# Scores of the first attention layer: eight 32x64 tiles of TensorE in place of four 32x128 tiles

## The chip, the cores and the metric

The kernel runs on one core of a Trainium2 chip. The metric is the device time of one execution in microseconds, and the median of several runs is compared. All data is float32.

## What is computed

The input is a batch of 8 images with 32x32 positions and 512 channels. Two residual attention layers follow each other. The first has 16 heads of 32 channels, the second 4 heads of 128 channels with relative position logits. The change concerns the first layer alone:

```python
# layer 0, N = 1024 tokens, 16 heads of 32 channels
x = x + _L0_conv_ref(_gn(x), w_qkv, w_proj, b_proj)

qkv = xt @ w_qkv
q, k, v = ...                                  # each (B, 16, N, 32)
attn = jnp.einsum('bhid,bhjd->bhij', q * 32 ** -0.5, k)   # the scores
attn = jax.nn.softmax(attn, axis=-1)
out = jnp.einsum('bhij,bhjd->bhid', attn, v)
out = out.transpose(...).reshape(B, N, C) @ w_proj + b_proj
```

## The kernel before

Activations are held transposed, with channels on the 128 partitions and the 1024 tokens along the free dimension. The 512 channels are four chunks of 128, and one chunk holds four heads of the first layer, each on 32 partitions of its own.

The attention of the first layer (`attention_0`) walks through `steps`: four chunks `m`, two halves `h` of 512 queries, and eight blocks `j` of 128 keys. That is 64 steps for an image and 512 steps in all. One step has two parts.

- `front` computes the scores of four heads (`HB` = 4) for 128 keys by 512 queries. Head `r` takes its channels from partitions 32r to 32r+31, so its matmul (line 522) uses 32 rows and all 128 columns of TensorE, and it writes its own PSUM bank `ps[:, r, :]`. The four heads occupy the four row groups of the array. Then one ScalarE exponential (line 530) reads all four banks and writes `e`. The `ps` tile of four banks exists once (`bufs=1`), so the scores of the next step wait for the exponential of this one.
- `back` belongs to the step before. It multiplies `e` by the values (line 541): four matmuls with 128 rows and 32 columns, one for each head, which together fill the 128 partitions of one accumulator `acc`. VectorE adds `e` into a running sum (lines 550 and 552). At the end of a row of eight blocks, `finish` forms the sums over the keys with four matmuls of 128 rows by 32 columns (line 562), and `normalise` divides.

The rest of TensorE's work is put between these steps by `side_by_side`: projections of this image, of the next one and of the last one, through `by_columns` (line 305). It cuts every projection into four matmuls of 128 rows by 32 columns, one for each column group of the array:

```python
for g in range(P // 32):
    columns = slice(32 * g, 32 * g + 32)
    ins = nc.tensor.matmul(
        out[columns, :], weights[:, columns], moving, ...
```

The position logits of the second layer (lines 598 and 605) are of the same shape of tile. The attention of the second layer (lines 637, 638 and 649) uses the whole array of 128 by 128 and stands in stretches of its own.

TensorE's order of instructions is thus: scores of a step (line 522), values of the step before (line 541), one or two projections (line 305), and again scores. In the profile a float32 matmul stands as two MATMUL records, each with a weight load (LDWEIGHTS, engine PEld) of its own: the four score matmuls of a step are eight records.

Of the kernel before, what the change touches and what calls it, by code (L numbers as in the profile page):

```python
# [17 lines left out]
P = 128  # L18
# [9 lines left out]
def quick_path(  # L28
# [23 lines left out]
    nc = tc.nc  # L52
# [5 lines left out]
    NB = 512  # L58
    NH = N // NB
    D0 = 32  # L60
    H1, D1 = 4, 128
    HB = P // D0
# [39 lines left out]
    for u in range(4):  # L102
        rows = slice(32 * u, 32 * u + 32)
# [378 lines left out]
    def normalise(dst, acc_sums, name):  # L482

        su = mem.tile([P, NB], F32, tag="rec", name=f"su_{name}", bufs=2)
        nc.scalar.copy(su, acc_sums)  # L488
        turned = mem.tile([P, NB], F32, tag="rec", name=f"tu_{name}", bufs=2)
        nc.vector.transpose(turned, su)  # L490
        few = turned.rearrange("p (t c) -> p t c", c=32)[:, :, 0]
        rec = mem.tile([P, NB // 32], F32, tag="few", name=f"rc_{name}", bufs=2)
        nc.vector.reciprocal(rec, few)
        at = check_at[0]
        check_at[0] += 1
        nc.vector.tensor_tensor_reduce(
            out=few,
            in0=few,
            in1=rec,
            op0=ALU.add,  # L500
            op1=ALU.max,
            scale=1.0,
            scalar=0.0,
            accum_out=checks[:, at : at + 1],
        )
        nc.vector.transpose(  # L506
            su.rearrange("p (t c) -> p t c", c=32),
            rec.unsqueeze(2).to_broadcast([P, NB // 32, 32]),
        )
        nc.gpsimd.tensor_tensor(dst, dst, su, op=ALU.mult)  # L510

    def attention_0(q, k, v, b):

        steps = [(m, h, j) for m in (0, 2, 1, 3) for h in range(NH) for j in range(NT)]
        state = {}

        def front(m, h, j):
            name = f"0_{b}_{m}_{h}_{j}"
            ps = psum.tile([P, HB, NB], F32, tag="ps", name=f"ps_{name}", bufs=1)
            for r in range(HB):  # L520
                rows = slice(r * D0, (r + 1) * D0)
                nc.tensor.matmul(  # L522
                    ps[:, r, :],
                    k[m][rows, j * P : (j + 1) * P],
                    q[m][rows, h * NB : (h + 1) * NB],
                    start=True,
                    stop=True,
                )
            e = mem.tile([P, HB, NB], F32, tag="e0", name=f"e_{name}", bufs=2)
            nc.scalar.activation(e, ps, AF.Exp, scale=D0 ** -0.5)  # L530
            return e

        def back(m, h, j, e):
            name = f"0_{b}_{m}_{h}_{j}"
            if j == 0:
                state["acc"] = psum.tile([P, NB], F32, tag="acc", name=f"acc_{name}", bufs=1)
                state["first"] = e
            acc = state["acc"]
            for r in range(HB):
                c0 = (m * HB + r) * D0  # L540
                nc.tensor.matmul(  # L541
                    acc[r * D0 : (r + 1) * D0, :],
                    v[:, j, c0 : c0 + D0],
                    e[:, r, :],
                    start=(j == 0),
                    stop=(j == NT - 1),
                )
            if j == 1:
                state["esum"] = mem.tile([P, HB, NB], F32, tag="es0", name=f"es_{name}", bufs=1)
                nc.vector.tensor_add(state["esum"], state["first"], e)  # L550
            elif j > 1:
                nc.vector.tensor_add(state["esum"], state["esum"], e)  # L552
            if j < NT - 1:
                return
            nc.scalar.copy(q[m][:, h * NB : (h + 1) * NB], acc)
            state["ended"] = (m, h, state["esum"])

        def finish(m, h, esum):
            name = f"0_{b}_{m}_{h}"
            su = psum.tile([P, NB], F32, tag="acc", name=f"sums_{name}", bufs=1)  # L560
            for r in range(HB):
                nc.tensor.matmul(  # L562
                    su[r * D0 : (r + 1) * D0, :],
                    ones[:, :D0],
                    esum[:, r, :],
                    start=True,
                    stop=True,
                )
            normalise(q[m][:, h * NB : (h + 1) * NB], su, name)

        pending = None
        for at in steps:
            if "ended" in state:
                finish(*state.pop("ended"))
            e = front(*at)
            if pending is not None:
                back(*pending)
            pending = (*at, e)
            yield 2
        back(*pending)  # L580
        yield 1
        finish(*state.pop("ended"))
# [832 lines left out]
```

## Time and profile before

| What | Value |
|---|---|
| Median of 5 runs | 3923.36 us (3921.57 to 3928.71) |
| Profiled execution, time | 3921.98 us |
| Profiled execution, span | 3920.1 us |
| Mean granted TensorE clock | 0.996 |
| Busy: TensorE matmul / weight load | 3810.7 us / 1415.5 us |
| Busy: VectorE / ScalarE / GpSimd | 2523.0 / 1721.9 / 615.6 us |
| Line 522, scores | 4096 matmul records, 590.7 us busy |
| Line 541, values | 4096 matmul records, 548.6 us busy |
| Line 530, exponential | 512 instructions, 961.9 us busy |

The page's first part gives the time in which each engine was busy, and its share of the span. PE is the matmul and PEld the weight load, which has an engine row of its own because it can run beside a matmul. Part 5 groups instructions by line and shape. A shape such as `32*128` means 32 rows by 128 columns of the array. The number after the bar is the busy time of the whole group as a union of its records, then the mean duration of one record in ns. Records that run at the same time each count with their full duration in the mean, so the mean times the count is more than the busy time. The timeline merges neighbouring records of a kind: it gives the start, the length from the first start to the last end, and the count.

### The profile page before, as it was taken

What the parts mean: (1) busy time and instruction counts of PE and PEld (TensorE: products, weight loads), DVE (VectorE), ACT (ScalarE), POOL (GpSimd) and SP (SyncE); (2) the same over time, 40 slices, a digit from 0 to 9 for tenths busy, and PEclk for the clock granted to TensorE, in tenths of its full rate; (3) what the DMA queues carried; (4) which work ended last, traced back from release to release, by engine and by line L of the source; (5) the groups of instructions that cost most, each with busy time, mean ns of one, the idle gap of its engine ahead of it and who ended that gap; (6) DMA issues with size and microseconds to landing.
All of it is one profiled execution on the core that took longest, in us unless ns stands there. A gap on an engine that the chain in (4) does not pass through costs nothing.

```text
span 3920.1 us, 71583 instructions
## 1 busy us (share of the span) xinstructions
PE 3810.7 (97%) x30338; PEld 1415.5 (36%) x30338; DVE 2523.0 (64%) x2915; ACT 1721.9 (44%) x1761; POOL 615.6 (16%) x396
## 2 busy tenths in 40 slices
PE   6999899999999999999999999999999999999998
PEld 3222244232443324432343323433234332344353
DVE  5777775577745867458664686656865568654544
ACT  1555553444434454344544445344453445643232
POOL 1341001121111210112101121111200112011101
PEclk9999999999999999999999999999999999999999
DMA  6231120133201422023120241103311123110401
GB/s 167 72 110 41 47 60 6 39 115 70 60 2 53 116 59 55 10 89 84 46 54 16 92 94 38 44 24 97 88 44 32 31 91 69 31 63 21 120 17 23
DMA packets 498694, 234.18 MB, mean 60 GB/s; under 512 B 286368, under 2 KB 478144, under 8 KB 497344
## 3 DMA queue, kind: packets, MB, share of 16 engines
q1 hardware_dynamic: 495232, 214.79, 20.5%
q0 software_dynamic: 2608, 13.70, 0.9%
q8 instruction: 241, 3.95, 0.4%
q10 hardware_dynamic: 528, 1.05, 0.1%
q14 instruction: 85, 0.70, 0.1%
HBM read 170.72 MB, written 58.72 MB: 59 GB/s over the span
## 4 chain that ended last, share of the span: by engine, by line
PE 85%; DVE 8%; ACT 3%; issue 2%; POOL 1%; DMA 1%; SPq 1%; DVEq 0%; POOLq 0%; ACTq 0%
PE ps L522 12%; PE ps L637 11%; PE acc L649 11%; PE acc L541 10%; PE y_k L305 4%; PE y_q L305 4%; PE y_v L305 4%; PE ps L638 3%; PE x_v L305 3%; PE z_k L305 3%; PE x_k L305 3%; PE x_q L305 3%; PE z_v L305 3%; PE z_q L305 3%; ACT e L530 2%; DVE es L552 2%
## 5 line engine op out<-in xcount | busy, mean ns | idle before, releaser
L530 ACT ACTIVATE e<-ps 128x2048 f32<-128x2048 f32 x512 | 961.9, 1879 | 842.2 <-PE ps L522 643.1
L552 DVE TENSOR_TENSOR es<-es,e 128x2048 f32<-128x2048 f32 x384 | 888.3, 2313 | 402.8 <-ACT e L530 400.5
L522 PE MATMUL ps<-q,k 32*128 32x512 f32 x4096 | 590.7, 642 | 33.4 <-ACT e L530 33.2
L640 ACT ACTIVATE e<-ps 128x512 f32<-128x512 f32 x512 | 305.7, 597 | 586.4 <-PE ps L638 549.9
L541 PE MATMUL acc<-e,v 128*32 128x512 f32 x4096 | 548.6, 607 | 0.4 <-ACT su L488 0.4
L637 PE MATMUL ps<-q,k 128*128 128x512 f32 x1024 | 523.8, 593 | 0.3 <-DVE posT L623 0.3
L649 PE MATMUL acc<-e,v 128*128 128x512 f32 x1024 | 522.0, 593 | 0.0
L660 DVE TENSOR_TENSOR es<-es,e 128x512 f32<-128x512 f32 x384 | 291.6, 759 | 265.0 <-ACT e L640 263.7
L510 POOL TENSOR_TENSOR q<-q,su 128x512 f32<-128x512 f32 x128 | 214.3, 1674 | 1567.9 <-DVE su L506 1567.1
L638 PE MATMUL ps<-posT,sel 128*128 128x512 f32 x512 | 406.9, 795 | 0.0
L522 PEld LDWEIGHTS ps<-q,k 32*128 32x128 f32 x4096 | 161.7, 183 | 428.9 <-ACT e L530 213.3
L637 PEld LDWEIGHTS ps<-q,k 128*128 128x128 f32 x1024 | 194.0, 190 | 245.7 <-issue 240.2
L649 PEld LDWEIGHTS acc<-e,v 128*128 128x128 f32 x1024 | 193.6, 190 | 146.2 <-issue 104.8
L541 PEld LDWEIGHTS acc<-e,v 128*32 128x32 f32 x4096 | 81.9, 108 | 385.7 <-issue 341.2
L550 DVE TENSOR_TENSOR es<-e,e 128x2048 f32<-128x2048 f32 x64 | 175.1, 2735 | 38.9 <-ACT e L530 38.9
L490 DVE STREAM_TRANSPOSE tu<-su 128x512 f32<-128x512 f32 x128 | 90.6, 708 | 135.9 <-ACT su L488 135.7
L638 PEld LDWEIGHTS ps<-posT,sel 128*128 128x128 f32 x512 | 97.5, 190 | 122.2 <-issue 122.2
L488 ACT COPY su<-sums 128x512 f32<-128x512 f32 x128 | 74.9, 585 | 149.5 <-PE sums L562 81.5
L658 DVE TENSOR_TENSOR es<-e,e 128x512 f32<-128x512 f32 x64 | 44.2, 690 | 145.7 <-ACT e L640 145.7
L623 DVE TENSOR_TENSOR posT<-pp,posT 32x512 fp32r<-32x512 f32 x128 | 111.8, 873 | 32.0 <-ACT posT L618 30.7
L618 ACT CAST posT<-pp 32x512 fp32r<-32x512 f32 x128 | 105.9, 827 | 45.1 <-PE pp L605 43.9
L414 POOL TENSOR_TENSOR k<-b_k,p_k 128x512 f32<-128x512 f32 x32 | 50.6, 1583 | 477.3 <-ACT p_k L379 477.3
(188 smaller groups left out, 4507.7 us busy)
## 6 DMA issues: line engine op xcount, KB each, us to landing
w_qkv<-ws_qkv SPq DMA_DIRECT2D x168, 128.0 KB, 2.5
xs<-in_x SPq DMA_DIRECT2D x256, 64.0 KB, 2.5
d<-x0T SPq DMA_DIRECT2D x32, 512.0 KB, 3.4
x1T<-d SPq DMA_DIRECT2D x32, 512.0 KB, 5.1
d<-x1T SPq DMA_DIRECT2D x32, 512.0 KB, 3.4
x2T<-d SPq DMA_DIRECT2D x32, 512.0 KB, 5.6
out<-ot SPq DMA_DIRECT2D x256, 64.0 KB, 2.0
w_qkv<-in_L_conv_w_qkv SPq DMA_DIRECT2D x126, 128.0 KB, 2.2
```

The costliest lines, as they stand in the source:

```text
L305: ins = nc.tensor.matmul(out[columns, :], weights[:, columns], moving, start=start, stop=stop, skip_group_check=open_sum,)
L510: nc.gpsimd.tensor_tensor(dst, dst, su, op=ALU.mult)
L522: nc.tensor.matmul(ps[:, r, :], k[m][rows, j * P : (j + 1) * P], q[m][rows, h * NB : (h + 1) * NB], start=True, stop=True,)
L530: nc.scalar.activation(e, ps, AF.Exp, scale=D0 ** -0.5)
L541: nc.tensor.matmul(acc[r * D0 : (r + 1) * D0, :], v[:, j, c0 : c0 + D0], e[:, r, :], start=(j == 0), stop=(j == NT - 1),)
L550: nc.vector.tensor_add(state["esum"], state["first"], e)
L552: nc.vector.tensor_add(state["esum"], state["esum"], e)
L637: nc.tensor.matmul(ps, k[h][:, keys], q[:, h, queries], start=True, stop=False)
L638: nc.tensor.matmul(ps, sel[:, keys], posT[:, h, queries], start=False, stop=True)
L640: nc.scalar.activation(e, ps, AF.Exp, scale=1.0 / math.sqrt(D1))
L649: nc.tensor.matmul(acc, v[:, j, h * D1 : (h + 1) * D1], e, start=(j == 0), stop=(j == NT - 1),)
L660: nc.vector.tensor_add(state["esum"], state["esum"], e)
```

## The change

Each head's 128 keys are taken in two halves of 64. The score matmul of a head becomes two, each with 32 rows and 64 columns of the array, which write partitions 0 to 63 and 64 to 127 of the same PSUM bank. The first halves of all four heads are issued first, then the second halves. Operands, results and the exponential after them are the same.

```diff
@@ -517,15 +517,18 @@
         def front(m, h, j):
             name = f"0_{b}_{m}_{h}_{j}"
             ps = psum.tile([P, HB, NB], F32, tag="ps", name=f"ps_{name}", bufs=1)
-            for r in range(HB):
-                rows = slice(r * D0, (r + 1) * D0)
-                nc.tensor.matmul(
-                    ps[:, r, :],
-                    k[m][rows, j * P : (j + 1) * P],
-                    q[m][rows, h * NB : (h + 1) * NB],
-                    start=True,
-                    stop=True,
-                )
+            for i in range(2):
+
+                some = slice(64 * i, 64 * i + 64)
+                for r in range(HB):
+                    rows = slice(r * D0, (r + 1) * D0)
+                    nc.tensor.matmul(
+                        ps[some, r, :],
+                        k[m][rows, j * P + 64 * i : j * P + 64 * i + 64],
+                        q[m][rows, h * NB : (h + 1) * NB],
+                        start=True,
+                        stop=True,
+                    )
             e = mem.tile([P, HB, NB], F32, tag="e0", name=f"e_{name}", bufs=2)
             nc.scalar.activation(e, ps, AF.Exp, scale=D0 ** -0.5)
             return e
```

## The prediction

> **What bounds the kernel now.** I read the page's first part, then the chain that ended last, then the groups of instructions, then the timeline of one ordinary step.
>
> ```profile
> PE 3810.7 (97%) x30338; PEld 1415.5 (36%) x30338; DVE 2523.0 (64%) x2915; ACT 1721.9 (44%) x1761; POOL 615.6 (16%) x396
> ...
> PE 85%; DVE 8%; ACT 3%; issue 2%; POOL 1%; DMA 1%; SPq 1%; DVEq 0%; POOLq 0%; ACTq 0%
> ```
>
> TensorE is busy in 97% of the span and carries 85% of the chain that ended last. Nothing else comes near: VectorE has 64%. So what a step of scores costs on TensorE passes into the time nearly whole. But "busy" is not "streaming at full rate", and the groups show where it is not:
>
> ```profile
> L522 PE MATMUL ps<-q,k 32*128 32x512 f32 x4096 | 590.7, 642 | 33.4 <-ACT e L530 33.2
> ...
> L541 PE MATMUL acc<-e,v 128*32 128x512 f32 x4096 | 548.6, 607 | 0.4 <-ACT su L488 0.4
> ...
> L522 PEld LDWEIGHTS ps<-q,k 32*128 32x128 f32 x4096 | 161.7, 183 | 428.9 <-ACT e L530 213.3
> ...
> L541 PEld LDWEIGHTS acc<-e,v 128*32 128x32 f32 x4096 | 81.9, 108 | 385.7 <-issue 341.2
> ```
>
> Scores (L522) and values (L541) have the same count of matmul records of the same 512 columns, yet a score record is 35 ns longer in the mean. The two weight-load rows give the reason: a load of 128 columns takes 183 ns, one of 32 columns 108 ns. TensorE idled only 33 us before the scores for the exponential (L530), in 28 places; in the other steps `ps` is free in time.
>
> The timeline of TensorE, start and length in us, shows an ordinary step:
>
> ```profile
> 1307.35 0.61 PE L305 MATMUL z_wp<-q,w_p 128*32 128x512 f32 x4
> 1307.89 1.14 PE L522 MATMUL ps<-q,k 32*128 32x512 f32 x8
> 1308.96 1.07 PE L541 MATMUL acc<-e,v 128*32 128x512 f32 x8
> 1309.85 1.90 PE L305 MATMUL x_wp<-q,w_p 128*32 128x512 f32 x16
> ```
>
> and its weight loads:
>
> ```profile
> 1307.89 0.31 PEld L522 LDWEIGHTS ps<-q,k 32*128 32x128 f32 x8 [0.84 <-issue]
> 1308.96 0.16 PEld L541 LDWEIGHTS acc<-e,v 128*32 128x32 f32 x8 [0.76 <-issue]
> 1309.42 0.13 PEld L305 LDWEIGHTS x_wp<-q,w_p 128*32 128x32 f32 x4 [0.30 <-issue]
> 1309.85 0.13 PEld L305 LDWEIGHTS x_wp<-q,w_p 128*32 128x32 f32 x4 [0.30 <-issue]
> ```
>
> From the start of the scores to the start of the values are 1.07 us; from there to the projection, with as many records, only 0.89. The projection's loads return every 0.43 us, four at a time: that is one round, four column groups streaming 512 columns together. A step's scores and values are two such rounds each, 0.86 us. What lies above it is set-up.
>
> The single records of this step take the 1.07 us apart. The four first-pass matmuls last 692 ns, the four second-pass ones 588. The difference, 104 ns, is the first load of 128 columns, which nothing covers: the tile shape changes here from 128x32 to 32x128, and nothing of the new shape starts until the old one has drained. The second passes start 534 ns after the first ones: 427 of streaming and 107 of load. Neighbouring tiles start 7 ns apart, so the fourth is 20 ns behind the first. From the end of the last stream to the first load of the values pass another 88 ns, the drain. Sum: 107 + 427 + 427 + 20 + 88 = 1069, against 1071 read in nearly all 512 steps. For the values the same calculation gives 27 ns of open load (matmul records of 617 and 592), and no drain at the end because the projection has the same tile shape.
>
> **The change part by part.** It touches one line. The order of the instructions of the changed kernel has eight matmuls of 64x512 where four of 128x512 stood, in 512 steps. On TensorE, ScalarE and GpSimd all else keeps its order; on VectorE one statistics instruction changes places with a neighbour; on SyncE's queue a few loads of `xs`, issued four in a row, move past one other transfer each. There are no new waits or transfers, and ScalarE reads the same four banks behind the last matmul. So the sum has three terms, each times 512.
>
> 1. Streaming. Eight tiles of 32x64 fill the array as four of 32x128 did. If all eight stream together, a step is still two rounds of 427 ns: nothing gained or lost. The trace has four row tiles together (L522) and four column tiles together (L541, L305), but no shape cut both ways. Bounds: 0 if rows and columns are independent; two more rounds and a load, about 0.85 to 0.9 us a step, if the two halves of a head follow each other. I take 0. The Trainium skill ("TensorE: Matmul & The Clock Gate", Part 3) has a rule that speaks against it: a weight load overlaps running matmuls only where its row group differs. Each second-half tile has the row group of a first half, so by that rule its load would wait for that matmul, and the step would lose some 0.88 us, 450 us in all. The trace contradicts the rule: L541's four tiles share all 128 rows and differ in columns alone, and their eight loads are done within 0.16 us while the first matmuls have been running since 1308.96. The same part gives a 4x4 packing as 10.6 times faster than single tiles, which speaks for tiles cut both ways; no run here shows it.
>
> 2. The open load. It falls from 128 to 64 columns. By the rows: (183 - 108) / 96 = 0.78 ns a column, so 50 ns less; by the open part, 107 for 128 columns and 27 for 32 is 0.83 a column, so 53 less. Bounds: 0 (the two halves of a row group load one after the other) and -54. I take -53, for L541 shows four column tiles loading side by side: -53 x 512 = -27.1 us. The second-pass loads lie under the first streams and cost nothing before or after; their cover is 427 ns for some 130 ns.
>
> 3. The stagger. Eight tiles begin 7 ns apart, so the last is 47 ns behind the first, not 20, and the drain waits for it: +27 x 512 = +13.8 us. Bounds: 0 (the drain hides it) and twice the step between tiles, 13 ns, +73 a step. The row for it: four projection loads of about 110 ns span 0.13 us, so three steps make 0.02. The skill states a floor ("TensorE: Matmul & The Clock Gate", Part 1): starts of matmuls are never closer than about 25 ns. With it eight starts would take 175 ns, four 75, and the sum of terms 2 and 3 would be +47 a step, +24 us: slower. The records of L522 start 7 ns apart, so I take 7.
>
> The supply of instructions is not a limit by the trace: the scores become 32 records in about 1.04 us, and a projection with 256 columns (x_v, y_v in L305) takes 64 records in 1.73 us without a gap, 27 ns each.
>
> Sum: 0 - 27.1 + 13.8 = -13.3 us. In the 28 steps that wait for the exponential the loop is scores, exponential, scores, and shorter scores shorten it just as much, so nothing is taken off. The profiled execution took 3921.98 (span 3920.1): 3921.98 - 13.3 = 3908.7. The median of the runs stands 1.4 above it, so about 3910 is expected. About 0.2%, 8 us, is what a measurement of this kernel can tell from no change.
>
> **The rivals.**
>
> A, the forecast (0.65): all eight tiles together. Between 3895 (term 2 whole, stagger hidden) and 3920. For it: the free mixing of column tiles in L541 and L305. Against: no mixed tile is in the trace.
>
> B, the halves follow each other (0.18): the two tiles of a row group share one stream of `q`, or one load path, so the second half starts when the first has passed. Place: between i = 0 and i = 1 of line 522. Price: two rounds and a load of 64 columns, 854 + 53, less the 53 saved at the start, so 854 x 512 = +437 us: 4361. Scores would then bind TensorE by two more rounds a step, while ScalarE's exponential, 1.88 us a step, stays hidden. It decides from the point where the last tile starts more than 74 ns behind the first (53 saved and the 20 there are now). For it: a row group has so far never been used by two tiles at once; against: in L541 all row groups are, by four.
>
> C, no gain (0.17): the loads of the two halves share the row group's path, or tiles start up to 13 ns apart. Terms 2 and 3 cancel or turn to +20 ns a step: 3918 to 3934. For it: the stagger takes back half the gain as it is.
>
> That the change doesn't do what it says is excluded by the order of the instructions. VectorE as the new bound is excluded as well: a gain of 0.3% leaves it at 64%.
>
> **How the numbers follow.** The likeliest is A: 3910. The range 3893 to 3934 holds A and C, 0.82 of the chance, and leaves B out. Faster by over 0.2%: most of A and none of B, 0.60. Within: the edge of A and half of C, 0.13. Slower: the rest of C and B, 0.27.
>
> **What would show it.** Right: weight loads of L522 near 133 ns, 8192 of them; first-pass matmuls about 53 ns longer than second-pass ones, not 104; scores to values in 1.04 us, not 1.07; the eight first passes starting within 50 ns. Wrong: two groups of starts 0.4 us or more apart, scores to values near 1.9 us (B); or loads still near 183 ns or starts 13 ns apart (C).

## Result and profile after

The changed kernel takes 3915.95 us (median of 28 runs, 3910.45 to 3919.30), the kernel before 3922.91 us (48 runs, 3918.68 to 3928.71). The ratio is 0.9982 with a 95% interval of 0.9977 to 0.9987: about 7 us faster, with an interval from 5 to 9. The forecast was 13 us faster by 3910, in a range of 3893 to 3934. The direction is right and the size is half.

The page of the changed kernel, engines and the groups of the scores (now L525), of the values (L544) and of their weight loads:

```profile
span 3917.2 us, 79775 instructions
...
PE 3803.6 (97%) x34434; PEld 1370.8 (35%) x34434; DVE 2524.4 (64%) x2915; ACT 1722.1 (44%) x1761; POOL 616.5 (16%) x396
...
L525 PE MATMUL ps<-q,k 32*64 32x512 f32 x8192 | 578.0, 616 | 35.3 <-ACT e L533 35.2
...
L544 PE MATMUL acc<-e,v 128*32 128x512 f32 x4096 | 548.1, 607 | 0.4 <-ACT su L488 0.4
...
L525 PEld LDWEIGHTS ps<-q,k 32*64 32x64 f32 x8192 | 120.5, 130 | 432.1 <-ACT e L533 215.4
```

Twice as many score records as before take 578 us of TensorE in place of 591. A load of 64 columns takes 130 ns, which lies between the 183 of 128 columns and the 108 of 32. TensorE is still the bound.

The timeline of the same step as in the prediction, matmuls and then weight loads:

```profile
1308.25 0.61 PE L305 MATMUL z_wp<-q,w_p 128*32 128x512 f32 x4
1308.79 1.11 PE L525 MATMUL ps<-q,k 32*64 32x512 f32 x16
1309.84 1.06 PE L544 MATMUL acc<-e,v 128*32 128x512 f32 x8
1310.72 1.90 PE L305 MATMUL x_wp<-q,w_p 128*32 128x512 f32 x16
```

```profile
1308.79 0.23 PEld L525 LDWEIGHTS ps<-q,k 32*64 32x64 f32 x16 [0.84 <-issue]
1309.84 0.16 PEld L544 LDWEIGHTS acc<-e,v 128*32 128x32 f32 x8 [0.81 <-issue]
```

Scores to values are 1.05 us here, 1.07 before. All sixteen score loads are done within 0.23 us, so both halves of every head have their weights long before the first streams end. The single records give the sum exactly. In the middle of the run the eight first-pass matmuls start 2 to 49 ns after the first load, the eight second passes 480 ns behind the first ones (534 before), and the values 564 ns after that (537 before). Together this is 1044 ns against 1071, in practically every step that no wait or other work interrupts. Over 512 steps, 26.7 ns are 13.7 us.

So the scores gained what was forecast, and about half of it does not arrive in the time. Note also where the step stands: at 1308.79 in this profile, 0.9 us later than in the profile of before. By then 196 shorter steps had passed, which alone would have put it 5.2 us earlier. The experiments ask two things: whether the three terms of the step are what they were taken for, and where the rest went.

### The profile page after: what moved, and what is told of

Its sections match the earlier page's. It is cut to its first block, busy times and chain, and to the rows that moved or that the text cites. A ratio compares the mean times of both kernels' runs of the same rounds, so it can differ in the third digit from the quotient of the medians.

```text
span 3917.2 us, 79775 instructions
## 1 busy us (share of the span) xinstructions
PE 3803.6 (97%) x34434; PEld 1370.8 (35%) x34434; DVE 2524.4 (64%) x2915; ACT 1722.1 (44%) x1761; POOL 616.5 (16%) x396
## 3 DMA queue, kind: packets, MB, share of 16 engines
q10 hardware_dynamic: 528, 1.05, 0.1%
## 4 chain that ended last, share of the span: by engine, by line
PE 84%; DVE 9%; ACT 3%; issue 2%; POOL 1%; DMA 1%; SPq 0%; another core or an unknown queue 0%; DVEq 0%; ACTq 0%; POOLq 0%
PE ps L640 11%; PE acc L652 11%; PE ps L525 11%; PE acc L544 10%; PE y_k L305 4%; PE y_q L305 4%; PE y_v L305 4%; PE ps L641 3%; PE x_v L305 3%; PE z_k L305 3%; PE x_k L305 3%; PE x_q L305 3%; PE z_v L305 3%; PE z_q L305 2%; ACT e L533 2%; DVE es L555 2%
## 5 line engine op out<-in xcount | busy, mean ns | idle before, releaser
L525 PE MATMUL ps<-q,k 32*64 32x512 f32 x8192 | 578.0, 616 | 35.3 <-ACT e L533 35.2
L544 PE MATMUL acc<-e,v 128*32 128x512 f32 x4096 | 548.1, 607 | 0.4 <-ACT su L488 0.4
L525 PEld LDWEIGHTS ps<-q,k 32*64 32x64 f32 x8192 | 120.5, 130 | 432.1 <-ACT e L533 215.4
L544 PEld LDWEIGHTS acc<-e,v 128*32 128x32 f32 x4096 | 81.6, 108 | 414.0 <-issue 366.3
```

The source lines that it names most:

```text
L525: nc.tensor.matmul(ps[some, r, :], k[m][rows, j * P + 64 * i : j * P + 64 * i + 64], q[m][rows, h * NB : (h + 1) * NB], start=True, stop=True,
L544: nc.tensor.matmul(acc[r * D0 : (r + 1) * D0, :], v[:, j, c0 : c0 + D0], e[:, r, :], start=(j == 0), stop=(j == NT - 1),)
```

## Experiments

**Sixteen tiles of 32x32.** The open load should fall further, the stagger should grow.

```diff
-            for i in range(2):
-                some = slice(64 * i, 64 * i + 64)
+            for i in range(4):
+                some = slice(32 * i, 32 * i + 32)
...
-                        k[m][rows, j * P + 64 * i : j * P + 64 * i + 64],
+                        k[m][rows, j * P + 32 * i : j * P + 32 * i + 32],
```

> Each head's 128 keys in four quarters: sixteen score tiles of 32x32. Theory (open load 0.83 ns a column, tiles start 6.7 ns apart, all tiles stream together): the open load falls to 27 ns, the last of sixteen tiles starts 100 ns behind the first, so scores to values 27 + 427 + 427 + 100 + 88 = 1069 ns, as with four tiles of 32x128; the time is that of the kernel before less at most 2 us, and 11 us above it at most through more half-clock windows. Rival (the gain comes from finer tiles as such, the stagger is hidden): 1044 - 27 = 1017 ns a step, 14 us faster than the changed kernel. Rival (the loads of one row group share a path): open load of the last tile 107 ns, 1150 ns or more a step, 40 us slower.

Measured: 3933.15 us, ratio to before 1.0025 (1.0016 to 1.0034), about 11 us slower than before. The timeline of a step:

```profile
1320.00 1.16 PE L525 MATMUL ps<-q,k 32*32 32x512 f32 x32
1321.09 1.06 PE L544 MATMUL acc<-e,v 128*32 128x512 f32 x8
```

By the single records the step is 1087 ns in the median, 18 more than the 1069 expected. The second passes start 453 ns after the first ones, which is 427 of streaming and 26 to 27 of open load: that term is exact. The stagger is not. In a step read out record by record, the first fourteen tiles start 6 to 7 ns apart, the last two 15 and 16; the last second pass starts 116 ns behind the first one, not 100. The 7 ns of the prediction thus hold for fourteen tiles and not for sixteen. Why the last two start late was not tried. Both rivals fall: finer tiles are not better as such, and the loads of one row group do not queue. The whole distance to before, 11 us, is more than 512 x 16 ns = 8 us; the remaining 3 lie within the interval.

**The loops exchanged.** Both halves of a head are issued next to each other.

```diff
-            for i in range(2):
-                some = slice(64 * i, 64 * i + 64)
-                for r in range(HB):
-                    rows = slice(r * D0, (r + 1) * D0)
+            for r in range(HB):
+                rows = slice(r * D0, (r + 1) * D0)
+                for i in range(2):
+                    some = slice(64 * i, 64 * i + 64)
```

> The changed kernel with the two loops exchanged: both halves of a head are issued one after the other, so that two tiles of the same row group come next to each other. Theory (every tile runs on its own): nothing changes, first passes 6.7 ns apart, 1.044 us a step, the time of the changed kernel within 4 us. Rival (a weight load must wait for matmuls of its own row group): the second half of a head starts only behind the first, hundreds of ns later, hundreds of us slower in all.

Measured: 3914.37 us, ratio 0.9981 (0.9972 to 0.9990), the same as the changed kernel. The records of one step of its scores (durations min/median/max, then first and last start):

```profile
L524 PEld LDWEIGHTS ps<-q,k x16: 127/130/131, 1317.4 to 1317.5; 32*64 32x64 f32 x16
L524 PE MATMUL ps<-q,k x16: 587/613/638, 1317.4 to 1318.0; 32*64 32x512 f32 x16
```

All sixteen loads begin within 0.1 us, though each second half now stands right behind a first half on the same 32 rows. First starts are 6 to 7 ns apart and the step is 1044 ns. A first pass takes 638 ns and a second 587: 51 ns of open load. That a load has to wait for matmuls of its own row group, the rule weighed in the prediction, does not hold in this run.

**Both kernels again.** This gives three profiles of each kernel.

> The changed kernel once more, for a second profile. Theory: scores to values 1.044 us in every undisturbed step, 26.7 ns less than before; what the time lacks of 512 x 26.7 = 13.7 us lies in windows at half clock (37 us of them ahead of the end in the first profile, 24 in that of before) and in waits for VectorE, about 0.2 us an image. If half-clock windows are chance alone, their sum varies between profiles of one kernel by 10 us and more, and is not larger here than before in the mean; if the change causes them, it stays near 37 us.

> The kernel before once more, for a second profile. If half-clock windows are chance, their sum ahead of the end differs from the 24 us of the first profile by several us; if they are fixed by the program it is 24 us again. Scores to values 1.071 us.

> The changed kernel for a third profile: half-clock windows ahead of the end of 34 to 38 us if they come from the program's course, and a value below 31 in some profile if they are chance. A wait of 2.3 us for VectorE's b_k in the first image, seen in two profiles of it and in none of before, again if it belongs to the earlier arrival of TensorE.

> The kernel before for a third profile, for the half-clock windows ahead of the end (24 and 31 us so far). If they are chance alone, the three of before and the three of the changed kernel and its twin (37, 37, 34) should overlap; if the change adds to them, this one stays at or below 31.

Measured: the changed kernel 3914.58 us in eleven runs, ratio 0.9979 (0.9970 to 0.9988), and 3916.52 in the single later run; before 3924.74 and 3922.78 in single runs. With three profiles each, one can first read where the lead is lost. Up to the 97th exponential, which takes in the first image and half of the next, the steps alone should bring 2.6 us; before takes 509.9 to 510.0 us, the changed kernel 513.1, 512.9 and 510.0. In the 368 steps from the 97th to the 465th exponential, in which no profile of either has a half-clock window (explained below), before takes 2741.4 to 2741.5 us and the changed kernel 2733.7 to 2733.8. That is 7.7 us less, where the steps alone give 368 x 26.7 = 9.8: here 2.1 us are given back. In the last 47 steps it takes 211.4 to 211.5 us, against 210.6, 213.8 and 210.6 before. So in these profiles the beginning costs more than the long middle. Two causes can be read.

First, the waits of TensorE. The list of waits, before and then after (us in total, times, longest):

```profile
PE ps L522 <- ACT e L530: 33.2, 28, 7.6
...
PE y_wo L305 <- DVE a_wo L365: 10.9, 9, 1.7
```

```profile
PE ps L525 <- ACT e L533: 35.2, 29, 7.6
...
PE y_wo L305 <- DVE a_wo L365: 11.2, 9, 1.7
...
PE y_k L305 <- DVE b_k L373: 2.3, 1, 2.3
```

The wait for the exponential is 33.2 or 33.3 us in all three profiles of before, and 35.2, 35.1 and 35.7 after. One place of it comes back in five images, at the projection x_wo. The timeline there, first before and then after: the scores, VectorE's running sum, the exponential of these scores, and the next scores.

```profile
1825.90 1.14 PE L522 MATMUL ps<-q,k 32*128 32x512 f32 x8
...
1826.21 2.28 DVE L552 TENSOR_TENSOR es<-es,e 128x2048 f32<-128x2048 f32 x1
...
1828.59 1.88 ACT L530 ACTIVATE e<-ps 128x2048 f32<-128x2048 f32 x1 [5.11 <-DVE es L552]
...
1830.53 1.14 PE L522 MATMUL ps<-q,k 32*128 32x512 f32 x8 [0.78 <-ACT e L530]
```

```profile
1825.22 1.11 PE L525 MATMUL ps<-q,k 32*64 32x512 f32 x16
...
1825.72 2.28 DVE L555 TENSOR_TENSOR es<-es,e 128x2048 f32<-128x2048 f32 x1
...
1828.10 1.88 ACT L533 ACTIVATE e<-ps 128x2048 f32<-128x2048 f32 x1 [5.25 <-DVE es L555]
...
1830.03 1.12 PE L525 MATMUL ps<-q,k 32*64 32x512 f32 x16 [0.98 <-ACT e L533]
```

The exponential waits for VectorE's running sum to free its buffer, and TensorE for the exponential. The figure in brackets is all the idle time of ScalarE, most of it ahead of the scores: from their end to the exponential pass 1.55 us before and 1.77 after. In these two profiles the scores stand 0.68 us earlier than before, but the sum of VectorE only 0.49, so TensorE waits 0.98 us instead of 0.78. In the 368 steps all waits of TensorE add up to 13.4 us in each profile of before and 15.0 in each of the changed kernel: 1.6 of the 2.1 us. With 32x32 tiles, where TensorE comes later than before, they are 12.8 us, and the wait at x_wo is 0.70.

The wait for b_k, 2.3 us, falls into the first image. It stands in all three profiles of the changed kernel and in none of before, but not in that of the exchanged loops.

Second, the granted clock. It falls to half for windows of 3.41 us, up to three in a row. Leaving out the last 15 us of a run, they add up to 24, 31 and 24 us before, and to 37.5, 37.5 and 34 after. The sums do not overlap. A window full of matmuls costs up to half its length, 1.7 us, so the difference of 10 us costs up to 5. (The second profile of before has two windows in the last 47 steps where the others of before have none, and takes 3.2 us longer there.) The stages around two of these windows, first the first profile of before and then that of the changed kernel (columns: length, then busy time and count of PE, PEld, DVE, ACT and POOL, granted clock, DMA share, GB/s):

```profile
3295.00:3307.00 12.00, 9.38 (x80) 2.44 (x84) 11.63 (x13) 5.03 (x4) 3.15 (x1) 1.00 0.09 25
3464.00:3474.00 10.00, 7.40 (x86) 3.73 (x78) 7.21 (x11) 2.04 (x4) 2.54 (x2) 1.00 0.66 231
```

```profile
3290.00:3302.00 12.00, 9.34 (x88) 2.00 (x80) 11.63 (x13) 4.34 (x3) 3.15 (x1) 0.86 0.08 23
3460.00:3470.00 10.00, 7.41 (x88) 3.07 (x80) 6.66 (x10) 1.97 (x4) 1.27 (x1) 0.83 0.66 239
```

The same work, the same busy time of TensorE, the same two waits of 2.6 us in both kernels; and yet the clock is 1.00 before and 0.86 and 0.83 after. Window starts in a profile lie on a grid of 3.41 us. In the six profiles, 50 of the 55 half-clock windows counted here follow a cell of that grid in which TensorE was busy for 44% or less; the other five (49 to 71%) come right behind another half-clock window. The limit is not sharp: once a cell of 44% was not followed by one. The wait near 3294 fills most of one cell in the changed kernel (22% busy). In the first profile of before it starts at 3298.7 and lies across an edge (the cell from 3299.7 on is busy for 54%). In the second profile of before the same wait starts at 3299.0, the cell from 3299.6 on is busy for 40%, and the clock falls there too:

```profile
3295.00:3307.00 12.00, 9.39 (x68) 2.33 (x64) 11.64 (x13) 4.34 (x3) 3.16 (x1) 0.86 0.08 24
```

So such a window comes with the tiles of 32x128 as well. How much the clock took can be estimated by comparing runs of the same mean granted clock. At 0.995 the runs of before have a mean of 3924.3 us (27 runs) and those of the changed kernel 3914.0 (6 runs); at 0.996 it is 3921.0 (25) and 3910.5 (4). The distance is about 10.4 us at an equal clock and 7 over all, since 32 of 42 runs of the changed kernel had 0.994 and none of 52 of before. About 3 us are thus lost to the clock, and about 3 of 13.7 elsewhere. The clock is recorded to the thousandth only, which is about two windows, so this is a rough estimate.

**VectorE relieved.** In both kernels the running sum takes in two of the four heads from the third block on and leaves out the other two.

```diff
-                nc.vector.tensor_add(state["esum"], state["esum"], e)
+                nc.vector.tensor_add(
+                    state["esum"][:, :2], state["esum"][:, :2], e[:, :2]
+                )
```

> The kernel before with VectorE relieved: from the third block of keys on, the running sum of exponentials takes in two of the four heads alone (left out: the sums of the other two), so that 384 additions of 2313 ns become about half as long. It serves as the base for the next run. In itself: the waits of TensorE for the exponential (33 us) and for VectorE's results shrink; if they fed half-clock windows, those become fewer than the 24 and 31 us seen. Scores to values stay 1.071 us.

> The changed kernel with VectorE relieved in the same way (same sums left out). Theory (the part of the 13.7 us that the time lacks is given back where TensorE, now earlier, waits for the exponential that waits for VectorE's sum, and in half-clock windows after such waits): the distance to the run with four tiles of 32x128 grows from 7 us to 11 to 14, and the 0.2 us an image lost at the projection x_wo is gone. Rival (the missing part is lost elsewhere, in the supply of instructions or in transfers): the distance stays 7 us within 2.

Measured: 3895.58 us with four tiles (3893.44 to 3896.33), 3883.11 with eight (3880.44 to 3883.88). The distance is 12.5 us instead of 7 to 8. In the 368 steps it is 2727.3 - 2718.2 = 9.1 us, near the 9.8 of the steps alone. The waits of the relieved changed kernel:

```profile
PE ps L525 <- ACT e L533: 26.3, 21, 7.6
...
PE y_wo L305 <- DVE a_wo L365: 2.3, 2, 1.7
```

The wait at x_wo is gone, that for a_wo is 2.3 us in both relieved kernels, and that for the exponential differs by 1.0 us (25.3 with four tiles). In the 368 steps all waits add up to 1.9 and 2.1 us, so they differ by 0.2 us instead of 1.6. The rival, a loss in the supply of instructions or in transfers, falls. One part of the expectation failed: with four tiles the half-clock windows did not become fewer (27 us, counted as above, where 24 to 31 stood). With eight tiles they fell from 34 or more to 20.5 us, below those of four tiles. Part of the 12.5 us may therefore come from the clock.

**TensorE shifted.** This tests whether half-clock windows belong to the tile shape.

```diff
+        if b == 3:
+            late = bank("late", [P, P])
+            for _ in range(6):
+                nc.tensor.matmul(late, ones, ones, start=True, stop=True)
         rest, total = [], 0
```

> The changed kernel with six small matmuls (128x128, to a bank that nobody reads) ahead of the attention of the fourth image: TensorE runs some 1.5 to 1.8 us later from there on, without any other change. Theory (a half-clock window follows where a wait of TensorE fills most of one cell of a fixed grid of 3.41 us, so that windows are a matter of where the waits fall): the windows of the first image stay as they are (they lie ahead of the shift); of the two that follow the waits of 2.6 us near 3294 and 3462, the first disappears, because its wait now lies across the edge of two cells, about 1.0 and 1.6 us in each, and the second stays. Rival (the windows belong to the tile shape of the scores): both stay.

Measured, one run: 3912.14 us, within the range of the changed kernel (3910.45 to 3919.30) though below its median, although work was added. The windows, counted as above, add up to 27 us. Both of the windows in question are gone where the expectation has the second stay, and a third, near 3669, is gone too. The stages around the two, columns as above:

```profile
3290.00:3304.00 14.00, 11.34 (x124) 2.73 (x120) 13.63 (x14) 6.48 (x5) 3.16 (x1) 1.00 0.19 36
3461.00:3471.00 10.00, 9.80 (x78) 5.27 (x78) 7.21 (x12) 2.38 (x4) 1.27 (x1) 1.00 0.66 211
```

The shift was another than intended: the first 97 exponentials took 3.4 us less in this run than in the second profile of the changed kernel. The wait for b_k did not occur, and one half-clock window fell at 187 us instead of 225. So the first of the two waits fell 1.9 us earlier than in the first profile (at 3292.3) and the second 3.6 us earlier (at 3458.6), not later. The tile shape is the same and the windows are not, so they do not belong to the shape alone. That they follow from where waits fall on the grid fits all profiles shown, but a single run with an unintended shift is no proof of it.

**A version that relieves VectorE and leaves nothing out.** GpSimd takes the fourth head's part of the running sum, in all blocks from the third on or in every second one.

```diff
-                nc.vector.tensor_add(state["esum"], state["esum"], e)
+                nc.vector.tensor_add(
+                    state["esum"][:, :3], state["esum"][:, :3], e[:, :3]
+                )
+                nc.gpsimd.tensor_tensor(
+                    state["esum"][:, 3:], state["esum"][:, 3:], e[:, 3:], op=ALU.add
+                )
```

> The changed kernel with VectorE relieved without leaving anything out: from the third block on, GpSimd (16% busy) adds the fourth head's 512 columns to the running sum, VectorE the other three. Theory (TensorE gives time back where the exponential waits for VectorE's sum): VectorE's addition falls from 2.3 to about 1.8 us, and of the 31 us that half the sum was worth some 10 to 15 come: 3900 to 3906. Rival (GpSimd's addition, 1.7 us or more beside VectorE, holds e longer than VectorE did, or slows it): the wait of the exponential for e moves to GpSimd, no gain or a loss of some us.

> The same for every second block only: half the work on GpSimd. Theory: about half the gain of the run with all blocks, 3906 to 3912. If GpSimd is late because of its queue, this one is better than the other.

Measured: 3946.81 us for all blocks (ratio to before 1.0062, 1.0048 to 1.0076) and 3925.24 for every second one (1.0004, 0.9995 to 1.0013). Both are slower than the changed kernel, as the rival has it. The groups and the wait of the first:

```profile
L558 POOL TENSOR_TENSOR es<-es,e 128x512 f32<-128x512 f32 x384 | 939.5, 2447 | 609.3 <-ACT e L533 608.4
...
L555 DVE TENSOR_TENSOR es<-es,e 128x1536 f32<-128x1536 f32 x384 | 729.6, 1900 | 499.3 <-ACT e L533 496.6
```

```profile
PE ps L525 <- ACT e L533: 62.0, 33, 7.6
```

VectorE's addition fell to 1.90 us, near the 1.8 expected. GpSimd's takes 2.45 us in the mean for a quarter of the columns (1.25 in its shortest case), longer than VectorE took for all of them (2.3), so `e` is held longer. ScalarE's idle time ahead of the exponential that ends with one of these additions is 233 us instead of 186, with 20 us of it ended by GpSimd, and TensorE waits 62 us for the exponential instead of 35. The wait moved to GpSimd only in part; the rest of the increase ends with VectorE's own additions, and why was not tried. The half-clock windows of this run add up to 48 us. No complete version tried is faster than the changed kernel; the exchanged loops are its equal.

## Why the prediction was right in direction and half in size

Streaming (term 1, taken at 0). Right. Eight tiles cut both ways stream together: 427 ns for each pass, first passes within 47 ns. Rival B, 0.18 of the chance, falls.

The open load (term 2, taken at -53 ns). Right: second passes start 480 ns after the first ones in place of 534, and the 32x32 run continues the line with 453.

The stagger (term 3, taken at +27 ns). Right for eight tiles: 564 ns to the values in place of 537. For sixteen the 7 ns failed at the end, so it was luck that the spacing read from four tiles still held at eight. Rival C's late starts exist, but behind the fourteenth tile.

The sum of these, 13.3 us, was met by the records with 13.7.

The step that failed is the sentence that nothing is taken off in the waiting steps. It looked at the loop of scores and exponential, and not at what the exponential itself waits for. In the profile of before, the view already said it at x_wo: VectorE's sum ended the wait of the exponential. Where VectorE ends the wait, an earlier TensorE waits longer, and part of the lead is cut. In the 368 steps without a half-clock window 2.1 of 9.8 us are lost, 1.6 of them in longer waits. With VectorE relieved only 0.7 us are lost there, and the waits differ by 0.2. The chain that the prediction shows gave a sign of it: VectorE and ScalarE carry 8% and 3% of it.

A second term was missing altogether: the clock. The page shows it as tenths that are all nines, 0.996 in the mean; ahead of the end that is 24 us at half rate, and 34 to 37.5 in the changed kernel. Four such windows, at up to 1.7 us each, can take back half of a change of 13 us. Together the longer waits (about 2 us for the exponential, 0.3 for a_wo, 2.3 for b_k where it occurs) and the windows (up to 5 us) are large enough for the 6 to 7 us that are missing; the runs of equal clock put about 3 us on each side. The split differs from profile to profile and is not settled further. No run shows that the tile shape itself makes the windows more frequent; how the change comes to have more of them is argued from where the waits fall on the grid. Why b_k is late in some runs and not in others was not tried.

That the measured gain, 0.18%, lies so near the bound of 0.2% that the prediction set for "within" is the effect of these two losses; "within" had got a chance of 0.13.

## What to carry to other kernels

Read the cost of a tile shape from the records: exposed load, streaming, distance between the starts, drain. A cut into more tiles shortens the first and lengthens the third, so it has an optimum; here it is 64 columns, with 1044 ns against 1071 for 128 and 1087 for 32. Before summing a gain over all steps, look in the timeline for places where the bounding engine waits for something that will not come earlier by as much; part of the lead is cut at each of them. For changes below half a per cent, list the windows of reduced clock in several profiles of each kernel, and compare runs of the same granted clock, since the windows differ from one run to the next.

## What was not expected of the hardware

Starts of concurrent tiles were 6 to 7 ns apart for fourteen tiles in a row and 15 to 16 ns for the last two of sixteen. Two tiles on the same 32 rows load their weights 7 ns apart while matmuls of these rows begin. The clock fell to half for 3.41 us after single waits of 2.4 to 2.7 us that left TensorE busy for 22 to 40% of a cell of the grid, and the same waits left it at 1.00 in another run of the same kernel. A GpSimd addition of 512 columns took 2.45 us in the mean while VectorE was adding beside it, and 1.25 in its shortest case.
